# A perceiver block on one Trainium2 core: where the weights are quantised, two accumulator banks in the first unit, and the order of the drain

## The chip, the core and the metric

The kernel runs on one core of a Trainium2 chip. A core has a matrix engine (PE, with its weight loads shown apart as PEld), a vector engine (DVE), a scalar engine (ACT), a general engine (POOL) and a queue engine that mainly starts DMAs (SP). Each works through its own instructions in order and waits on semaphores for the others. Matrix products go to PSUM, which has eight banks of 128 x 512 floats; everything else lives in SBUF or in DRAM.

The metric is the time of one execution on the device, in microseconds (us). Three runs of the kernel before took 1754.26, 1755.36 and 1758.02 us; their median is 1755.36.

## The reference

The input is x (8 sequences of 64 rows, 512 wide) and a context (8 x 1601 rows, 256 wide). Three blocks follow each other, each with a residual sum:

```python
x = x + cross_attention(layernorm(x), ctx)       # 16 heads of 128; q and k normalised by RMS; softmax over 1601 keys
x = x + causal_self_attention(layernorm(x))      # 16 heads of 32
x = x + feed_forward(layernorm(x))               # 2048 wide, SiLU gate, RMS norm
```

The two weights of the feed-forward block are quantised inside the kernel, in groups of 64 along a row:

```python
w = w_fp32.astype(bfloat16); w_g = w.reshape(-1, 64)
scale = clip(mean(abs(w_g), axis=-1), 1e-08)
q = clip(round(w_g / scale), -1, 1)              # -1, 0 or 1
w_hat = q * scale;  w + (w_hat - w)              # the sum in bfloat16
```

## The kernel before

**Quantisation.** The two feed-forward weights are cut into 48 pieces of 128 x 512. For each piece `load_weights` (L332) loads it as floats into tile `wf` by SP; `magnitudes` (L343) makes |w| (`aw`) and sign(w) (`sg`) on ACT, in bfloat16; `quantise` (L350) makes the scales, the threshold mask `m`, mask times sign, and |w| - scale on DVE (tot, scl, thr, m, m, sg); `signed` (L369) finishes on DVE with two operations; `put_by` (L374) transposes the piece on DVE in blocks of 32 and sends it with four DMAs of SP to the DRAM tile `fw`. The feed-forward block reads `fw` back much later. The pieces are spread over the kernel wherever there is room: eight in the prologue, one for each pair of heads; in the main part one in the steps `q` = 0 and 4 of every unit, and in units 0 and 1 also in step 2; what is left, six, in the drain. The pool that holds `wf`, `aw`, `sg` and `m` has one buffer for each. It is `early` in the prologue and `fq` after it; `wpool[0]` names the one in use. The transposed piece is written over `aw`.

**Prologue.** Context tails and their key lengths first, then layer norm of x, then `two_heads(n)` (L505) for n = 0 to 8. It makes the queries of two heads with Strassen-Winograd products (q_u, q_2, q_5 in three banks), the copies p1, p5, u2 of partial sums on ACT, sums on DVE into `qraw` (L525, L533, L539), the lengths of the queries of the pair before (`query_roots`) and their products with the key weights (`score_weights`, tile `aps`, multiplied on DVE at L581). L539, the sum after the product of s3 and t3, must read q_u before the last product of the pair can use that bank. One piece is quantised within each call with n < 8; the load for the next call is issued after the call.

**Main part.** The cross attention runs in 16 units (8 sequences, 2 groups of 8 heads), each in six steps of 256 keys: 96 calls of `step(u, q)` (L1085). In a step PE forms the keys (seven products of 512 columns into banks p_u, p_5, p_2) to get their lengths, and the scores (seven of 256 columns, bank s_a); ACT squares the keys and sums them up (L741), DVE adds partial products (c12 L1158, c22 L1170, the quarters of the scores L1212 and L1222, c11 L1216). Scaling of the scores and the running maximum (`scale_pair`, L711, L727) are put off to the next step by the list `later`. Softmax and the weighted context of unit u - 1 run in the steps of unit u; its sums are gathered, inverted and divided in unit u + 1 (`find_sum`, `spread_sum`, `invert_sums`, `gather_first`, `gather`, `divide`). In unit 0 the steps 0 to 3 also hold the key lengths of the context tails for the second group (`tail_roots`, bank y0 or y1). PSUM has two banks m, and one each of k, s, y0, y1, y2 and y3. p_u takes bank k in every step; y0 to y3 hold the accumulators of the weighted context from unit 1 on.

**Drain.** After the last step: what is left of unit 14 (weighted context, gathering, division), the values of the first head group (`values`, tile `vp`), the softmax of unit 15 and its weighted context (L828), the rest of the pieces, and the loads of the weights that the later blocks need. Then the output projection (L1044), self attention and feed-forward.

**What sets the order.** In the prologue the instructions of PE, DVE and ACT run in the order in which the code writes them; in the main part POOL's too; from the drain on PE's alone. The other queues are ordered by the scheduler of the framework, with the semaphores for every dependency, a tile whose buffer is used again among them.

Of the kernel before, what the change touches and what calls it, by code (L numbers as in the profile page):

```python
# [19 lines left out]
P = 128  # L20
# [8 lines left out]
def perceiver_kernel(  # L29
# [313 lines left out]
    def magnitudes(wf):  # L343
        aw = wpool[0].tile([P, 8, 64], BF, tag="aw", name="aw")
        nc.scalar.activation(aw.rearrange("p g k -> p (g k)"), wf, AF.Abs)
        sg = wpool[0].tile([P, 8, 64], BF, tag="sg", name="sg")
        nc.scalar.activation(sg.rearrange("p g k -> p (g k)"), wf, AF.Sign)
        return aw, sg

    def quantise(u, aw, sg):  # L350
# [16 lines left out]
        return u, m, aw, sg  # L367

    def signed(u, m, aw, nd):  # L369
        nc.vector.tensor_tensor(nd, aw, nd, ALU.subtract)  # L370
        nc.vector.tensor_tensor(m, nd, m, ALU.mult)
        quantised[u] = m, aw

    def put_by(u):  # L374

        m, aw = quantised.pop(u)
        wT = aw.rearrange("p g k -> p (g k)")
        nc.vector.transpose(wT, m.rearrange("p g k -> p (g k)"))
# [10 lines left out]
    with tc.tile_pool(name="qphase", bufs=1) as qp, tc.tile_pool(  # L389
# [115 lines left out]
        def two_heads(n):  # L505
# [3 lines left out]
            if go:  # L509
# [14 lines left out]
                grow(q_2, a12, b21, True)  # L524
                nc.vector.tensor_tensor(qa[:, :NH], q_2, p1, ALU.add)  # L525
                grow(q_5, s1, t1, True)
                p5 = kept_q("qp5")
# [8 lines left out]
            if go:  # L536
                tern = quantise(n, *magnitudes(early.pop()))
                grow(q_u, s3, t3, False)
# [46 lines left out]
        with tc.manual_schedule(  # L585
# [72 lines left out]
            head_sums(0)  # L658
            early = [load_weights(0)]
            for n in range(H // 2 + 1):  # L660
# [5 lines left out]
                if n + 1 < H // 2:  # L666
                    early.append(load_weights(n + 1))
                if n == HG // 2:
# [7 lines left out]
    fq = xs.enter_context(tc.tile_pool(name="fq", bufs=1, side="right"))  # L676
    wpool[0] = fq

# [244 lines left out]

    def gather_first(u):

# [6 lines left out]
        nc.vector.tensor_tensor(p1, p6, p1, ALU.add)  # L932
        nc.gpsimd.tensor_tensor(cw[:, : W // 2], p1, p5, ALU.add)
        yG[u] = c15, cw

    def gather(u):

# [4 lines left out]
        (_, y12), (y21, y22) = outputs_of(u)  # L942
        add = nc.vector.tensor_tensor
        add(u3, p7, u2, ALU.add)
        add(y12, by_head(p4), by_head(u3), ALU.add)
        add(y21, by_head(p3), by_head(u4), ALU.add)
        add(u3, t22, u3, ALU.add)
        nc.gpsimd.tensor_tensor(y22, by_head(u3), by_head(p5), ALU.add)

    def divide(u):  # L950
        b, g = divmod(u, G)
        eng = nc.gpsimd if u < last - 1 else nc.vector
        for c in range(NC):
            y = a_sb[g][c][:, :, ts(b, S)]
            eng.tensor_tensor(y, y, rB[u], ALU.mult)

# [128 lines left out]
    def step(u, q):  # L1085
# [11 lines left out]
        fw_tile = None  # L1097
        tern = (q in TERN or u < 2 and q == 2) and n_q < NQ
        if tern:
            wf = load_weights(n_q)  # L1100


        p_u = bank("p_u", "k")
        product(p_u, a11, b11, True)
# [40 lines left out]
        if u > 1 and q == 2:  # L1145
            spread_sum(u - 2)
        if u == last and q == NQU - 1:
            spread_sum(last - 1)
        product(p_u, s2, t2_, False)
# [25 lines left out]
        if q == 1 and u > 1:  # L1175
            gather(u - 2)
        if u == last:
# [14 lines left out]
        if u > 1 and q in (2, 3):  # L1192
            for i in range(2):
                invert_sums(u - 2, 2 * (q - 2) + i)
        if u == last and q == NQU - 1:
            for i in range(4):
                invert_sums(last - 1, i)
        if n_tp < len(pairs) and turn_at[n_tp] == u * NQU + q:
# [27 lines left out]
        nc.scalar.copy(quarters[:, 2], s_a[:, 1])  # L1226
        squares(ssq[:, 0], 0, c11)
        if new:
            under_way = pair_products(*new)
            weigh(3)  # L1230
# [38 lines left out]
    with tc.manual_schedule(engines={mybir.EngineType.PE}):  # L1269
# [8 lines left out]
        prob_sums(last - 1, NQU - 1)  # L1278
        find_max(last)
        tail_products(last - 1)  # L1280
        mB[last] = spread_diag(mB[last])
        s_sb.pop((last - 1, NJF))
        under_way = pair_products(last - 1, NQU - 1)
        weigh(5)
        gather_first(last - 1)
        weigh(9)
        load_contexts(NU * NY)
        gather(last - 1)
        divide(last - 1)
        for h in range(HG // 2):  # L1290
# [533 lines left out]
```

## Time and profile before

| what | value |
|---|---|
| median of three runs | 1755.36 us |
| the profiled execution | 1753.64 us |
| its span, first to last instruction | 1751.8 us |
| mean granted clock of PE | 0.983 |
| PE, DVE, ACT, POOL busy | 95%, 74%, 66%, 59% |
| chain that ended last | PE 75%, DVE 9%, POOL 8%, ACT 4% |
| prologue's eight steps with a piece | 27.6 to 167.6 us |
| unit 0 | 178.0 to 254.9 us |
| last step, then drain | from 1418 us |

The span is cut into stages by the first products of each. A row of the timeline gives start, duration, engine, line, operation, the tile written and the tiles read, and in brackets how long the engine stood idle before and what released it. The busy share of PE is an average over stages with different limits. A granted clock under 1 means that PE ran at a lower rate for part of that stage.

### The profile page before, as it was taken

To read this page: it belongs to the slowest core of one execution; us is meant where nothing else is said; L and a number is where in the kernel's file an instruction comes from. 1 tells how busy PE (TensorE), PEld (TensorE's weight loads), DVE (VectorE), ACT (ScalarE), POOL (GpSimd) and SP (SyncE) were. 2 spreads that over 40 slices of the span, in tenths; PEclk is the share of its full clock that TensorE was granted. 3 is DMA by queue.
4 is the path that set the end of the run, shared out by engine and by line. 5 is a ranking of instruction groups with operands and counts; after the bars stand their busy time and mean duration, and the time that the engine had idled before them with its cause. 6 is when DMAs were issued, how large, how long until landed. Compare 5 with 4: busy or idle time off the path is not lost.

```text
span 1751.8 us, 22186 instructions
## 1 busy us (share of the span) xinstructions
PE 1671.6 (95%) x6068; PEld 1070.0 (61%) x6068; DVE 1293.2 (74%) x1937; ACT 1161.7 (66%) x4511; POOL 1027.8 (59%) x1240
## 2 busy tenths in 40 slices
PE   7768999999999999999999999999999988999999
PEld 4544446666666666666666666666666554466787
DVE  5555678888887878888888878888888878435641
ACT  4544778787777778787777878787777763113451
POOL 3120225687878697787878787787878771100031
PEclk9888999999999999999999999999999998999999
DMA  6111212121121121212121211121111116700340
GB/s 205 22 25 15 58 25 48 44 49 36 34 49 35 46 47 34 48 40 44 38 43 35 50 43 35 47 45 38 38 43 49 33 53 189 214 1 1 85 108 24
DMA packets 254243, 92.73 MB, mean 53 GB/s; under 512 B 208400, under 2 KB 234792, under 8 KB 254120
## 3 DMA queue, kind: packets, MB, share of 16 engines
q1 hardware_dynamic: 244762, 68.78, 17.7%
q0 software_dynamic: 8928, 22.02, 4.3%
q8 instruction: 48, 0.79, 0.2%
q14 instruction: 75, 0.61, 0.1%
q10 hardware_dynamic: 430, 0.53, 0.1%
HBM read 77.62 MB, written 7.34 MB: 49 GB/s over the span
## 4 chain that ended last, share of the span: by engine, by line
PE 75%; DVE 9%; POOL 8%; ACT 4%; issue 2%; DMA 1%; SPq 0%; DVEq 0%; ACTq 0%; POOLq 0%
PE p_u L737 15%; PE y L737 13%; PE p L737 11%; PE s_a L737 10%; PE gu L1635 3%; PE op L1044 3%; PE aps L580 2%; PE kp L302 2%; PE fop L1753 2%; PE s L737 2%; PE mm_qk L1430 2%; PE q_u L481 2%; PE q L481 1%; PE vp L1029 1%; POOL den L870 1%
## 5 line engine op out<-in xcount | busy, mean ns | idle before, releaser
L741 ACT ACTIVATE c<-c 128x128 f32<-128x128 f32 x1152 | 341.7, 302 | 94.3 <-DVE c L1170 70.5
L741 ACT ACTIVATION_READ_ACCUMULATOR c<-c 128x1 f32 x1152 | 220.9, 192 | 0.0
L737 PE MATMUL p_u<-wk,cxT 128*128 128x512 f32 x384 | 197.0, 594 | 6.5 <-ACT p_u L741 6.5
L711 DVE TENSOR_TENSOR s<-s,ssq 128x1024 f32<-128x1024 f32 x96 | 130.6, 1360 | 54.9 <-ACT ssq L105 54.9
L737 PE MATMUL y<-s,cxn 128*128 128x256 f32 x540 | 146.8, 381 | 0.0
L727 DVE TENSOR_TENSOR mx<-mx,s 128x512 f32<-128x512 f32 x160 | 137.3, 858 | 5.5
L737 PEld LDWEIGHTS s_a<-aT,cxS 128*128 128x128 f32 x384 | 73.5, 192 | 92.8 <-issue 81.7
L800 DVE TENSOR_TENSOR s<-s,mB 128x1024 f32<-128x1024 f32 (+1 forms) x102 | 125.4, 1241 | 1.6 <-ACT mB L778 1.6
L865 POOL TENSOR_TENSOR yT<-s 128x256 f32<-128x256 f32 x76 | 82.9, 1091 | 69.2 <-PE y L737 67.3
L741 ACT ACTIVATE p_u<-p_u 128x128 f32<-128x128 f32 x384 | 100.4, 262 | 27.2 <-PE p_u L737 18.1
L737 PE MATMUL s_a<-aT,cxS 128*128 128x256 f32 x384 | 115.1, 382 | 0.0
L804 ACT ACTIVATE s<-s,zero_t 128x1024 f32<-128x1024 f32 (+1 forms) x102 | 112.0, 1099 | 4.3 <-DVE s L800 4.3
L737 PE MATMUL s_a<-aT,cxT 128*128 128x256 f32 x384 | 114.3, 379 | 0.0
L737 PEld LDWEIGHTS y<-s,cxn 128*128 128x128 f32 x540 | 103.4, 191 | 14.6
L737 PE MATMUL p_u<-wkS,cxT 128*128 128x512 f32 x192 | 101.1, 608 | 5.9 <-DVE c L1170 5.9
L737 PEld LDWEIGHTS s_a<-aT,cxT 128*128 128x128 f32 x384 | 72.8, 190 | 51.2 <-issue 40.9
L1137 ACT COPY p<-p 128x512 f32<-128x512 f32 x96 | 56.2, 585 | 69.9 <-PE p L737 68.2
L737 PE MATMUL p_u<-wkS,cxS 128*128 128x512 f32 x192 | 99.7, 601 | 1.4 <-POOL cxS L230 1.4
L737 PE MATMUL p<-wkS,cxS 128*128 128x512 f32 x192 | 99.3, 599 | 1.4 <-POOL cxS L228 1.4
L737 PE MATMUL p<-wk,cxS 128*128 128x512 f32 x192 | 99.1, 598 | 0.0
L737 PE MATMUL p<-wk,cxT 128*128 128x512 f32 x192 | 98.0, 592 | 0.0
L1170 DVE TENSOR_TENSOR c<-p_u,p 128x512 f32<-128x512 f32 x96 | 63.7, 664 | 41.1 <-PE p_u L737 41.0
(272 smaller groups left out, 4338.7 us busy)
## 6 DMA issues: line engine op xcount, KB each, us to landing
cxn<-in_ctx_dram SPq DMA_DIRECT2D x96, 256.0 KB
cxB<-in_ctx_dram SPq DMA_DIRECT2D x192, 64.0 KB
wf<-in_L_ffn_w_gate_up_dram SPq DMA_DIRECT2D x32, 256.0 KB
fgu<-fw POOLq DMA_DIRECT2D x4, 2048.0 KB, 8.4
fw<-aw SPq DMA_DIRECT2D x192, 32.0 KB
wq<-in_L_xattn_Wq_dram SPq DMA_DIRECT2D x4, 1024.0 KB
wf<-in_L_ffn_w_proj_dram SPq DMA_DIRECT2D x16, 256.0 KB
wo<-in_L_xattn_Wo_dram POOLq DMA_DIRECT2D x16, 256.0 KB, 5.6
```

The lines of the kernel that those rows point to most:

```text
L481: nc.tensor.matmul(out_, a[:, c], b[:, c], start=first, stop=True, skip_group_check=not first)
L711: nc.vector.tensor_tensor(flat, flat, kr.unsqueeze(2).to_broadcast([P, 2 * HG, S]), ALU.mult)
L727: nc.vector.tensor_tensor(mx[u][:r], mx[u][:r], s[:r], ALU.max)
L737: nc.tensor.matmul(out_, a, w, start=start, stop=True, skip_group_check=not start)
L741: nc.scalar.activation(k[:, ts(h, HD)], k[:, ts(h, HD)], AF.Square, accum_out=ssq[:, 4 * half + h : 4 * half + h + 1],)
L800: nc.vector.tensor_tensor(t, t, m.to_broadcast([r, len(js), W]), ALU.subtract)
L804: nc.scalar.activation(t, t, AF.Exp, bias=zero_t[: t.shape[0]], scale=1.0)
L865: eng.tensor_tensor(s1, a21, a22, ALU.add)
L1044: nc.tensor.matmul(op, o_sb[h][:, ts(t, P)], wo_sb[h], start=(h == 0), stop=(h == H - 1),)
L1137: nc.scalar.copy(p5, p_5)
L1170: nc.vector.tensor_tensor(c22, p_u, p5, ALU.add)
L1635: nc.tensor.matmul(gu[:, cols], fgu_sb[rr // 8][:, rr % 8, c, :], xs_[n_][c][:, cols], start=(c == 0 and n_ == 0), stop=(c == ND - 1 and n ...
```

## The change

1. *Prologue.* `magnitudes` moves out of `two_heads`: it is called with the load, after the call before. `quantise` moves forward, to just after the first sum on DVE (L525). The transposed piece no longer goes over `aw`, but over `wf`, seen as bfloat16 (`wT`), as long as `wpool` has one entry.
2. *After the prologue.* `wpool` has two entries, so `aw` and `sg` get two buffers; the transposed piece goes over `aw` as before.
3. *Unit 0.* Every step takes a piece, six in place of three, so three are left for the drain. p_u takes bank y2 in odd steps of unit 0.
4. *Gathering.* `gather` adds y21 first and is a generator; in the steps it is run through at once. `gather_first` and `gather` take the engine for their one addition on POOL as an argument.
5. *Last step.* `spread_sum` and `invert_sums` of unit 14 move to the end of step (15, 5).
6. *Drain.* `find_max` and `spread_diag` of unit 15 move behind the products with the tails and three of the last seven products of unit 14. Gathering runs wholly on DVE and in two halves, each divided by itself (`divide_half`), the first ahead of the last product.

```diff
     def magnitudes(wf):
-        aw = wpool[0].tile([P, 8, 64], BF, tag="aw", name="aw")
+        n = len(wpool)
+        aw = wpool[0].tile([P, 8, 64], BF, tag="aw", name="aw", bufs=n)
         nc.scalar.activation(aw.rearrange("p g k -> p (g k)"), wf, AF.Abs)
-        sg = wpool[0].tile([P, 8, 64], BF, tag="sg", name="sg")
+        sg = wpool[0].tile([P, 8, 64], BF, tag="sg", name="sg", bufs=n)
         nc.scalar.activation(sg.rearrange("p g k -> p (g k)"), wf, AF.Sign)
-        return aw, sg
+        return aw, sg, wf.bitcast(BF)[:, :512] if n == 1 else aw.rearrange("p g k -> p (g k)")
...
     def put_by(u):
-        m, aw = quantised.pop(u)
-        wT = aw.rearrange("p g k -> p (g k)")
+        m, wT = quantised.pop(u)
         nc.vector.transpose(wT, m.rearrange("p g k -> p (g k)"))
...
                 nc.vector.tensor_tensor(qa[:, :NH], q_2, p1, ALU.add)
+                tern = quantise(n, *early.pop())
                 grow(q_5, s1, t1, True)
...
             if go:
-                tern = quantise(n, *magnitudes(early.pop()))
                 grow(q_u, s3, t3, False)
...
-            early = [load_weights(0)]
+            early = [magnitudes(load_weights(0))]
...
-                    early.append(load_weights(n + 1))
+                    early.append(magnitudes(load_weights(n + 1)))
...
-    wpool[0] = fq
+    wpool = [fq, fq]
...
+        add(y21, by_head(p3), by_head(u4), ALU.add)
+        yield
         add(u3, p7, u2, ALU.add)
         add(y12, by_head(p4), by_head(u3), ALU.add)
-        add(y21, by_head(p3), by_head(u4), ALU.add)
         add(u3, t22, u3, ALU.add)
-        nc.gpsimd.tensor_tensor(y22, by_head(u3), by_head(p5), ALU.add)
+        eng.tensor_tensor(y22, by_head(u3), by_head(p5), ALU.add)
...
+    def divide_half(u, j):
+        for y in [o[j] for o in outputs_of(u)]:
+            nc.vector.tensor_tensor(y, y, rB[u][:, 4 * j : 4 * j + 4], ALU.mult)
...
-        tern = (q in TERN or u < 2 and q == 2) and n_q < NQ
+        tern = (q in TERN or u == 1 and q == 2 or u == 0) and n_q < NQ
...
-        p_u = bank("p_u", "k")
+        p_u = bank("p_u", "y2" if u == 0 and q % 2 else "k")
...
-        if u == last and q == NQU - 1:
-            spread_sum(last - 1)
         product(p_u, s2, t2_, False)
...
-        if u == last and q == NQU - 1:
-            for i in range(4):
-                invert_sums(last - 1, i)
...
         squares(ssq[:, 0], 0, c11)
+        if u == last and q == NQU - 1:
+            spread_sum(last - 1)
+            for i in range(4):
+                invert_sums(last - 1, i)
...
-        find_max(last)
         tail_products(last - 1)
-        mB[last] = spread_diag(mB[last])
         s_sb.pop((last - 1, NJF))
         under_way = pair_products(last - 1, NQU - 1)
-        weigh(5)
-        gather_first(last - 1)
+        weigh(3)
+        find_max(last)
+        mB[last] = spread_diag(mB[last])
+        weigh(2)
+        gather_first(last - 1, nc.vector)
+        weigh(1)
+        g_last = gather(last - 1, nc.vector)
+        next(g_last)
+        divide_half(last - 1, 0)
         weigh(9)
         load_contexts(NU * NY)
-        gather(last - 1)
-        divide(last - 1)
+        for _ in g_last:
+            pass
+        divide_half(last - 1, 1)
```

More of the change, by code (lines that the diff above doesn't have):

```diff
@@ L343, in magnitudes, with quantise @@
     def magnitudes(wf):
-        aw = wpool[0].tile([P, 8, 64], BF, tag="aw", name="aw")
+        n = len(wpool)
+        aw = wpool[0].tile([P, 8, 64], BF, tag="aw", name="aw", bufs=n)
         nc.scalar.activation(aw.rearrange("p g k -> p (g k)"), wf, AF.Abs)
-        sg = wpool[0].tile([P, 8, 64], BF, tag="sg", name="sg")
+        sg = wpool[0].tile([P, 8, 64], BF, tag="sg", name="sg", bufs=n)
         nc.scalar.activation(sg.rearrange("p g k -> p (g k)"), wf, AF.Sign)
-        return aw, sg
-    def quantise(u, aw, sg):
+        return aw, sg, wf.bitcast(BF)[:, :512] if n == 1 else aw.rearrange("p g k -> p (g k)")
+    def quantise(u, aw, sg, wT):
         tot = small.tile([P, 8], F32, tag="tot", name="tot")
@@ L366, in quantise, with signed @@
         )
-        return u, m, aw, sg
-    def signed(u, m, aw, nd):
+        return u, m, aw, sg, wT
+    def signed(u, m, aw, nd, wT):
         nc.vector.tensor_tensor(nd, aw, nd, ALU.subtract)
         nc.vector.tensor_tensor(m, nd, m, ALU.mult)
-        quantised[u] = m, aw
+        quantised[u] = m, wT
     def put_by(u):
-        m, aw = quantised.pop(u)
-        wT = aw.rearrange("p g k -> p (g k)")
+        m, wT = quantised.pop(u)
         nc.vector.transpose(wT, m.rearrange("p g k -> p (g k)"))
@@ L922, in by_head, with gather_first @@
         return t.rearrange("p (h s) -> p h s", s=S)
-    def gather_first(u):
+    def gather_first(u, eng=nc.gpsimd):
         y0, y1 = yps[u][:2]
@@ L932, in gather_first, with gather @@
         nc.vector.tensor_tensor(p1, p6, p1, ALU.add)
-        nc.gpsimd.tensor_tensor(cw[:, : W // 2], p1, p5, ALU.add)
+        eng.tensor_tensor(cw[:, : W // 2], p1, p5, ALU.add)
         yG[u] = c15, cw
-    def gather(u):
+    def gather(u, eng=nc.gpsimd):
         c15, cw = yG.pop(u)
@@ L943, in gather @@
         add = nc.vector.tensor_tensor
+        add(y21, by_head(p3), by_head(u4), ALU.add)
+        yield
         add(u3, p7, u2, ALU.add)
         add(y12, by_head(p4), by_head(u3), ALU.add)
-        add(y21, by_head(p3), by_head(u4), ALU.add)
         add(u3, t22, u3, ALU.add)
-        nc.gpsimd.tensor_tensor(y22, by_head(u3), by_head(p5), ALU.add)
+        eng.tensor_tensor(y22, by_head(u3), by_head(p5), ALU.add)
     def divide(u):
         b, g = divmod(u, G)
-        eng = nc.gpsimd if u < last - 1 else nc.vector
         for c in range(NC):
             y = a_sb[g][c][:, :, ts(b, S)]
-            eng.tensor_tensor(y, y, rB[u], ALU.mult)
+            nc.gpsimd.tensor_tensor(y, y, rB[u], ALU.mult)
+    def divide_half(u, j):
+        for y in [o[j] for o in outputs_of(u)]:
+            nc.vector.tensor_tensor(y, y, rB[u][:, 4 * j : 4 * j + 4], ALU.mult)
     def find_sum(u):
@@ L1175, in step @@
         if q == 1 and u > 1:
-            gather(u - 2)
+            list(gather(u - 2))
         if u == last:
```

## The prediction

> **What bounds the kernel now.** I read the page first: the span and the busy shares.
>
> ```profile
> span 1751.8 us, 22186 instructions
> ...
> PE 1671.6 (95%) x6068; PEld 1070.0 (61%) x6068; DVE 1293.2 (74%) x1937; ACT 1161.7 (66%) x4511; POOL 1027.8 (59%) x1240
> ```
>
> TensorE is the bound of the main part, where the change does little. Its places have less PE: the prologue (27 to 178 us), unit 0 (178 to 254) and the drain (from 1418). Next, busy time by stage, a prologue step and two of unit 0 (length, then PE, PEld, DVE, ACT, POOL, clock, DMA):
>
> ```profile
> 99.40:116.60 17.20, 12.91 (x45) 8.34 (x44) 9.70 (x19) 8.36 (x16) 2.84 (x4) 0.90 0.14 23
> 191.40:204.90 13.50, 12.73 (x36) 6.70 (x36) 9.61 (x17) 9.91 (x46) 1.79 (x4) 1.00 0.13 20
> 204.90:218.40 13.50, 12.73 (x36) 6.70 (x36) 8.88 (x15) 10.91 (x48) 1.79 (x4) 1.00 0.29 50
> ```
>
> A prologue step leaves PE idle for 4 us, a step of unit 0 for 0.8. The table of waits names both:
>
> ```profile
> PE q_u L481 <- DVE qraw L539: 30.0, 7, 5.4
> ...
> PE p_u L737 <- ACT p_u L741: 4.7, 5, 1.5
> ```
>
> The timeline shows the prologue's order: the first load, issued at 35.53, releases ACT 2.87 us later; PE waits for L539, which stands on DVE behind the quantisation; the transpose (L378) and then its four stores come at the step's end, and the next step's first copy (L523) starts 0.55 us after the transpose has ended.
>
> ```profile
> 38.40 0.63 ACT L345 ACTIVATE aw<-wf 128x512 bf16<-128x512 f32 x1 [6.59 <-DMA wf<-in_L_ffn_w_gate_up_dram]
> ...
> 110.47 1.13 PE L481 MATMUL q_u<-xS,wq 128*128 128x256 f32 x4 [4.29 <-DVE qraw L539]
> ...
> 116.48 0.71 DVE L378 STREAM_TRANSPOSE aw<-m 128x512 bf16<-128x512 bf16 x1
> ...
> 117.74 0.37 ACT L523 COPY qp<-q_u 128x256 f32<-128x256 f32 x1 [4.42 <-PE q_u L481]
> ```
>
> In the drain, PE's three long waits, and what a store takes: transpose ends at 1506.09, ACT is released at 1510.35.
>
> ```profile
> 1427.86 0.47 PE L110 MATMUL bp<-denh,ones_r 128*128 128x512 f32 x1 [4.14 <-DVE st L699]
> ...
> 1444.83 0.66 PE L784 MATMUL tp_mx<-ident,mx 128*128 128x128 f32 x4 [3.79 <-DVE mx L727]
> ...
> 1456.99 5.08 PE L1029 MATMUL vp<-a,wv 128*128 128x512 f32 x8 [3.38 <-DVE a L955]
> ...
> 1510.35 0.63 ACT L345 ACTIVATE aw<-wf 128x512 bf16<-128x512 f32 x1 [1.00 <-DMA fw<-aw]
> ```
>
> The sum is made against the profiled run: 1753.64 us, of which 1751.8 are span; it is 1.7 below the median, 1755.36.
>
> **Prologue.** Two edits pull against each other. The DVE part of a quantisation goes ahead of two adds, so L539 no longer holds up PE: that frees the 4.29 us wait. But Abs and Sign become the last ACT instructions before the next step's first copy, and the transposed result now goes into wf, which has one buffer. So load n+1 must wait for the stores of piece n, Abs for the load, and behind Abs on ACT stand all three copies that PE and DVE need. What covered load and stores before was most of a step; now nothing covers them.
>
> Call T the end of the transpose and p the start of the step's first copy. T to p now: stores 4.26 (1506.09 to 1510.35; 4.42 after 1516.62), load 2.75 (2.87 in the row; packets of later loads end about 2.3 after issue, plus the 0.4 seen at 38.40), Abs and Sign 1.06 (38.40 to 39.46), 0.05 for the semaphore: 8.1 against 0.55.
>
> p to T, at full clock: copy 0.45; DVE: add 0.42, quantisation 3.0 (39.06 to 42.06), two adds 0.95, so the last group of q_u starts at 4.85 (PE's own groups take 4.1 from copy, 65.43 to 69.56, and are ready at 4.6). From there: group 0.86, two aps 1.9, second multiply 0.65, two sign operations 0.92, transpose 0.71: 5.05. Sum 9.9. But PE has then stood idle for some 6 us (its three early groups end 2.2 after T; the copy lands at 8.5), and its groups come back slow: after 8.97 us idle at 42.53 three groups took 1.45, 1.71 and 1.37 instead of 0.86, 1.95 lost; at 92.22 (5.37 idle) the way from group to T took 7.76 instead of 5.05, 2.7 lost. I take 2.3, of which 2.0 reach the path: p to T is 11.9. The Trainium skill's page "TensorE: Matmul & The Clock Gate", section "Part 1: The HAM clock gate", says that an idle window of about 3.4 us halves the clock until some 3.4 us of work have passed, and so speaks against an edit that opens such a gap; by its figure the loss would be an estimated 1.7 a step and the prologue some 4 us shorter than my sum.
>
> So a period is 8.1 + 11.9 = 20.0; before it was (151.56 - 46.35)/6 = 17.5. Step 0: its load still lands at 38.40, so its first copy moves from 28.85 to 39.46, and the second step's p from 46.35 to about 55.2: +8.85. Six periods: +15.0. The last step has no load behind it and gains 17.1 - 11.9 = 5.2. Prologue: **+18.7**. Bounds: +3.3 if the clock never drops (period 18.0), +26 with stores and load at 9 and p to T at 12.2.
>
> **Unit 0.** A second bank frees PE from waiting for the squares of p_u: 0.79, 0.80, 0.80, 0.79, 1.47 and 0.80 us at the six step ends, 5.45 in all. The three extra pieces cost ACT 1.06 each, which fits into waits of 1.44 before L310, and DVE 4.5 each (signs and transpose 1.55, quantisation 2.95). From the quarter add (L1222) to the c12 add (L1158) DVE now has 4.85 + ssq 0.6 + scale 1.25 + two maxima 1.4 = 8.1; before 7.9 in steps 1 to 3. There PE still gains about 0.9 a step. In steps 4 and 5 there is no key work: L1158 came 6.3 after the quarter add and now comes 7.5 after it; the piece at the end of step 5 puts 2.9 of DVE ahead of the scores that find_max waits for. These two give back some 2.5. I take **-1**; bounds -5.45 and +3 (one quantisation that nothing hides). The three stores more per unit (2.6 us of SP each) lie in steps where SP is idle half of the time.
>
> **Main part.** The order in gather is new in 14 units: y21 first needs POOL's add, 0.73 to 1.57 long from 346.1, and the gather starts at 348.8: hidden. Should it not be, 14 x 0.5.
>
> **Last step and drain.** spread_sum moves to the end of step (15, 5): PE goes on at 1423.6 instead of waiting for denl. DVE still has scale, maxima and tail until 1428.4, so L1158 comes at 1428.4 instead of 1431.45, and without the reciprocals (3.38) ahead of it L1170 at 1429.1 instead of 1435.35: the step's PE work ends some 6 us earlier. The reciprocals now stand after the squares of c11, wait for the copy of rB (about 1435.2), end at 1438.6, and behind them on DVE stand the signs, transpose (1.5), scale (1.25) and maxima (1.5): tp_mx at about 1442.9, only 1.9 earlier. That is the new wait, some 4.7 us, behind which now stand only four products and not tail plus seven. Then gather_first on DVE (copy 0.6, three adds 1.2), y21 0.4, two half divisions 0.85: values start at about 1448.7 instead of 1456.99, -8.3, if the first four heads need only their half; if they wait for both halves, 2.5 later. Of the slow and broken first heads (5.08 instead of 3.44, 0.58, 0.74) I count 1.7 as gone, since three pieces fewer stand among DVE's copies. Together **-10**; bounds -6 and -14. Later the loads of context (PE waits 1.89 at 1485.64) follow the buffers and shift with them.
>
> Sum: 1753.64 + 18.7 - 1 - 10 = 1761.3.
>
> **Rivals.**
> A. The clock holds through the new wait, so p to T is 9.9: prologue +3.3, sum 1746. For it: the groups at 110.47 and 127.66 took 1.13 and 1.17 after 4.29 idle. Against: both steps still show 0.90, and 42.53 shows half rate. It turns to faster where the prologue costs under 7.5, a period under about 18.4.
> B. The drain gives nothing: tp_mx waits as long as before behind the reciprocals and both halves are waited for. Then -1 to -3 there: 1769 to 1771. For it: the chain on DVE is only 1.9 shorter.
> C. Unit 0 gives its full 5.4 and the drain 14, at +18: 1753, no change. Against: DVE's 8.1.
> D. The load does not wait for the stores, so the edit does more than I read: seven waits of 4.29 go, -30 there before step 0's +7: about 1720. Against: one buffer.
>
> **How the numbers follow.** Forecast 0.42 (own range 1757 to 1766), A 0.17, B 0.20, C 0.16, D 0.05. The band of 0.2% is about 3.5 us, the spread of the three runs and about what a measurement of this kernel can tell. Slower: 0.40 of the forecast and B, 0.60. Same: 0.02 and 0.14 of C, 0.16. Faster: A, D and 0.02 of C, 0.24. The range 1747 to 1772 leaves out D, most of A and the top of B.
>
> **What would show it.** Prologue: ACT idle 7 to 8 us before L345, released by the load; no PE wait for L539; periods near 20; PEclk lower. Unit 0: no PE wait for p_u; L1158 later after the quarter add. Drain: no wait before bp; tp_mx waiting over 3 us; vp near 1449 plus the earlier shift. The forecast falls if prologue periods are under 18.4 or the drain's waits stay.

## The result and the profile after

The changed kernel takes 1767.52 us (median of three runs, 1765.85 to 1769.82) against 1755.36 us before; the ratio is 1.0067, with a 95% interval of 1.0042 to 1.0093. It is slower by 0.7%. (One execution of the first run with whole divisions, below, took 4452 us and is left out of its times.) The profiled execution is the longest of the three, 1769.82 us, 16.2 us above the profiled one of before, and all stage times below are from that pair. The page of the kernel after: its span, busy time by engine, and the granted clock in 40 slices, in tenths (slice 2 stands at 7 where it was 8; slices 3 and 4 stand at 8 as before; the 8 that stood in the drain, in slice 34, is gone).

```profile
span 1768.0 us, 22174 instructions
...
PE 1673.8 (95%) x6068; PEld 1075.4 (61%) x6068; DVE 1291.5 (73%) x1941; ACT 1158.3 (66%) x4511; POOL 1022.7 (58%) x1238
...
PEclk9788999999999999999999999999999999999999
```

TensorE's busy time as a whole has hardly changed (1671.6 before), but that is a sum of two opposites: from 27.6 us to the start of unit 0 it is 118.3 instead of 110.5, with a granted clock of 0.82 instead of 0.86, and in the drain it is less. The rest of the loss is in waits. Setting each step of the two traces beside its counterpart shows where the 16.2 us arise; the shift is how much later the same instruction starts.

| place | shift there | what the stage added | forecast |
|---|---|---|---|
| unit 0 begins (178.0 before, 202.3 after) | +24.2 | prologue +24.2 | +18.7 |
| step (1,3), after the last extra piece's work | +26.6 | units 0 and 1 +2.4 | -1 |
| tail product of the last step (L690) | +26.1 | 13 units between: -0.4 | 0 |
| second group of the out-projection (L1048) | +15.8 | last step and drain -10.3 | -10 |
| end of the execution | +16.2 | +0.4 | 0 |

In the prologue the timeline shows the order that was forecast: the transpose into wf, its four stores, the load that waits for them, Abs, and only then the step's first copy, for which TensorE has been waiting.

```profile
110.31 0.71 DVE L378 STREAM_TRANSPOSE wf<-m 128x512 bf16<-128x512 bf16 x1
...
111.05 2.59 SPq L381 DMA_DIRECT2D fw<-wf  x4
...
115.31 0.33 SPq L340 DMA_DIRECT2D wf<-in_L_ffn_w_gate_up_dram  x1
118.02 0.63 ACT L346 ACTIVATE aw<-wf 128x512 bf16<-128x512 f32 x1 [7.56 <-DMA wf<-in_L_ffn_w_gate_up_dram]
...
119.07 0.35 ACT L523 COPY qp<-q_u 128x256 f32<-128x256 f32 x1
...
119.57 2.04 PE L481 MATMUL q_u<-xS,wqS 128*128 128x256 f32 x4 [6.24 <-ACT qp L523]
```

The transpose ends at 111.02 and the first copy starts at 119.07: 8.05 us. The load is issued at 115.31, 4.3 after the transpose. The group at 119.57 takes 2.04 us where one at full clock takes 1.03; the granted clock is 0.50 from 118.5 to 125.3. Two lines of the table of waits (sum, times, longest) and two steps by stage (length; PE, PEld, DVE, ACT, POOL; clock) give the size over the prologue:

```profile
ACT aw L346 <- DMA wf<-in_L_ffn_w_gate_up_dram: 61.9, 8, 10.3
...
PE q_u L481 <- ACT qp L523: 45.4, 7, 7.2
```

```profile
99.00:118.90 19.90, 14.08 (x44) 9.77 (x44) 9.24 (x18) 7.83 (x16) 4.03 (x5) 0.84 0.10 21
119.30:139.20 19.90, 14.17 (x44) 9.81 (x44) 9.86 (x19) 7.76 (x16) 4.59 (x8) 0.84 0.12 20
```

The old wait for L539 is gone, a longer one stands in its place, the clock of a step fell from 0.90 to 0.84, and TensorE is busy for 14.1 us of a step instead of 12.9. Step (1,0) is where the units lose most. Before, and then after: the step's first product, the root that ends the key norms, the scaling, and the transposed maxima.

```profile
254.68 1.13 PE L737 MATMUL p_u<-wk,cxT 128*128 128x512 f32 x2 [0.80 <-ACT p_u L741]
...
256.77 0.31 ACT L105 ACTIVATE ssq<-ssq,zero_t 128x16 f32<-128x16 f32 x1
...
257.12 1.23 DVE L711 TENSOR_TENSOR s<-s,ssq 128x1024 f32<-128x1024 f32 x1 [1.26 <-ACT ssq L105]
...
259.85 0.66 PE L784 MATMUL tp_mx<-ident,mx 128*128 128x128 f32 x4 [0.17 <-DVE mx L727]
```

```profile
277.21 1.02 PE L737 MATMUL p_u<-wk,cxT 128*128 128x512 f32 x2
...
280.14 0.67 PE L737 MATMUL s_a<-aT,cxS 128*128 128x256 f32 x2 [1.05 <-ACT s L1225]
...
281.87 0.31 ACT L105 ACTIVATE ssq<-ssq,zero_t 128x16 f32<-128x16 f32 x1
...
282.52 1.22 DVE L711 TENSOR_TENSOR s<-s,ssq 128x1024 f32<-128x1024 f32 x1
...
285.25 0.66 PE L784 MATMUL tp_mx<-ident,mx 128*128 128x128 f32 x4 [0.98 <-DVE mx L727]
```

From the step's start to the maxima it is 8.0 instead of 5.2 us: ACT's roots end 2.6 later, and on DVE a quantisation (from 279.27) ends just as the scaling could start, so both engines are late together. TensorE pays for it in three waits: 1.05 for ACT's copy of the scores, which stands behind the squares, 0.45 for its copy at L1116 (neither stood there before), and 0.98 for the maxima (0.17 before). Last, the drain after. No wait stands before the sums' bank; the maxima still wait, and the values start at 1475.08, which is 18.1 later than before where the step began 26.1 later.

```profile
1470.13 1.08 PE L784 MATMUL tp_mx<-ident,mx 128*128 128x128 f32 x4 [3.73 <-DVE mx L727]
...
1475.08 1.10 PE L1033 MATMUL vp<-a,wv 128*128 128x512 f32 x2 [0.89 <-DVE a L959]
1476.65 6.28 PE L1033 MATMUL vp<-a,wv 128*128 128x512 f32 x14 [0.48 <-DVE a L959]
```

### The profile page after: what moved, and what is told of

Same layout as the page of the kernel before. It is cut to its first block, busy times and chain, and to the rows that moved or that the text cites. A ratio compares the mean times of both kernels' runs of the same rounds, so it can differ in the third digit from the quotient of the medians.

```text
span 1768.0 us, 22174 instructions
## 1 busy us (share of the span) xinstructions
PE 1673.8 (95%) x6068; PEld 1075.4 (61%) x6068; DVE 1291.5 (73%) x1941; ACT 1158.3 (66%) x4511; POOL 1022.7 (58%) x1238
## 4 chain that ended last, share of the span: by engine, by line
PE 66%; DVE 12%; POOL 9%; ACT 6%; issue 4%; DMA 3%; SPq 1%; DVEq 0%; POOLq 0%; ACTq 0%
PE p_u L737 13%; PE y L737 11%; PE p L737 9%; PE s_a L737 9%; PE gu L1644 3%; PE op L1048 3%; PE q_u L481 2%; PE fop L1762 2%; PE mm_qk L1439 2%; PE s L737 2%; ACT c L741 2%; DVE s L711 2%; PE vp L1033 2%; DMA wf<-in_L_ffn_w_gate_up_dram 1%; ACT p_u L741 1%
## 5 line engine op out<-in xcount | busy, mean ns | idle before, releaser
L865 POOL TENSOR_TENSOR yT<-s 128x256 f32<-128x256 f32 x76 | 77.1, 1014 | 69.5 <-PE y L737 68.2
```

The costliest lines, as they stand in the source:

```text
L865: eng.tensor_tensor(s1, a21, a22, ALU.add)
```

## The experiments

My theory: most of the loss is the prologue's, because the load waits for the stores and TensorE's clock falls in the wait; units 0 and 1 lose because of the extra pieces, not the second bank; the drain gives 10. The rivals stand in each expectation. Ratios are to the kernel before, on the same chip. In the later tables "drain" is the time from the tail product of the last step to the second group of the out-projection; it is 99.21 before and 88.86 after. About half of that difference is the clock: in these stretches TensorE's busy time falls from 84.99 to 79.96 for the same work, and its granted clock rises from 0.93 to 0.98.

**The prologue's old order.**

```diff
-        return aw, sg, wf.bitcast(BF)[:, :512] if n == 1 else aw.rearrange("p g k -> p (g k)")
+        return aw, sg, aw.rearrange("p g k -> p (g k)")
...
-                tern = quantise(n, *early.pop())
...
+                tern = quantise(n, *magnitudes(early.pop()))
                 grow(q_u, s3, t3, False)
...
-            early = [magnitudes(load_weights(0))]
+            early = [load_weights(0)]
...
-                    early.append(magnitudes(load_weights(n + 1)))
+                    early.append(load_weights(n + 1))
```

> The changed kernel with the prologue's order of before: the load is taken up in the middle of the step, the transposed piece lies in aw. My theory (the prologue costs 24.2 us in the two traces, unit 0 and 1 together 2.4, and the drain gives 10): unit 0 begins within 1 us of 178.0, its first step of unit 2 comes 2 to 3 us later than before, the whole is 1753.6 + 2.4 - 10 = 1746, a ratio of 0.995 to the kernel before. Rival: the slower part lies behind the prologue (the drain gives nothing by itself and the profiled 10 us are a shift that the late start made possible): 1756, ratio 1.001.

Measured: 1744.9 us, ratio 0.9947 (0.9930 to 0.9964); expected 1746. Unit 0 begins at 176.7, 1.3 before the 178.0 of the kernel before where within 1 was expected, and the drain takes 88.63, as in the changed kernel. The rest of the change is thus a gain of some 0.5% by itself, and the prologue is what turns it into a loss; the rival falls.

**The load freed of the stores.** The signed piece goes into aw and is transposed into m; nothing is larger, and wf is free as soon as Sign has read it.

```diff
-        return aw, sg, wf.bitcast(BF)[:, :512] if n == 1 else aw.rearrange("p g k -> p (g k)")
+        return aw, sg, None if n == 1 else aw.rearrange("p g k -> p (g k)")
...
+        if wT is None:
+            nc.vector.tensor_tensor(aw, nd, m, ALU.mult)
+            quantised[u] = aw, m.rearrange("p g k -> p (g k)")
+            return
```

> The changed kernel, but in the prologue the signed piece goes into aw and is transposed into m, so that the next load needs no store to have ended; it still stands behind the issue of four stores on SP's queue. My theory (load waits for the stores of the piece): from the end of the transpose to the first copy 2.6 for the four issues, 2.75 for the load and 1.06 for Abs and Sign = 6.4 instead of 8.05, period some 18.4 instead of 20.3, the whole 1767.5 - 13 = 1754. Rival (the load starts when it does for another reason, the queue or the order on ACT): the period stays at 20.3, 1767.

Measured: 1712.3 us, ratio 0.9760 (0.9745 to 0.9774): some 54 us under the changed kernel, where I expected 13. The timeline of this version:

```profile
85.10 0.71 DVE L382 STREAM_TRANSPOSE m<-aw 128x512 bf16<-128x512 bf16 x1
...
85.84 2.59 SPq L385 DMA_DIRECT2D fw<-m  x4
85.85 0.63 ACT L346 ACTIVATE aw<-wf 128x512 bf16<-128x512 f32 x1 [1.30 <-DVE m L382]
...
86.91 0.35 ACT L527 COPY qp<-q_u 128x256 f32<-128x256 f32 x1
...
88.54 0.55 SPq L340 DMA_DIRECT2D wf<-in_L_ffn_w_gate_up_dram  x1
```

Abs waits for DVE's transpose alone; the load that it reads was there long before. I had left the load behind the issue of the four stores. But SP's order is not written by hand in this kernel. Once the load needed no store, the planner (the framework's scheduler) put the second load ahead of the first stores on SP, and every later load comes a step early. The period is 12.6 us (74.36, 86.91, 99.47), the clock of a step 1.00, and unit 0 begins near 145 instead of 202. So the theory's cause held (with the wait for the stores all of the loss goes, and more), and its size failed: it took SP's order as fixed.

**The load issued a step ahead by hand**, on the version with the freed load.

```diff
             early = [magnitudes(load_weights(0))]
+            ahead = [load_weights(1)]
...
-                    early.append(magnitudes(load_weights(n + 1)))
+                    early.append(magnitudes(ahead.pop()))
+                if n + 2 < H // 2:
+                    ahead.append(load_weights(n + 2))
```

> As the one before, and the load of piece n+1 is issued at the beginning of step n, when Sign of piece n has read wf, so that neither stores nor load stand between the transpose and the first copy; Abs and Sign keep their place ahead of the first copy. My theory: transpose to first copy about 1.2, TensorE is then the bound of a step (12.9 us busy), period 13.2 to 14.0, first copy still near 40, unit 0 begins near 155, the whole 1767.5 - 47 = 1720. Rival (the two places on ACT are the cost, or the stores now hold up the comparison that writes m): period 16 or more, the whole above 1740.

Measured: 1713.0 us, ratio 0.9762 (0.9747 to 0.9778), period 12.6 (86.0, 98.5, 111.3 at Abs); expected 1720 and 13.2 to 14.0. The same SP order as in the run before, and the same time: this says again that the first copy needs only the transposed piece out of the way. The rival (1740 or more) falls. Abs and Sign ahead of the copies cost nothing measurable here: TensorE's waits behind the first step are 8.9 us for L543 (7 waits) and 1.1 for the first copy.

**TensorE kept busy in the wait, too long**, by products whose result nothing reads, in the changed kernel.

```diff
+                if n > 0:
+                    idle_products(13, [P, 4, P])
```

> The changed kernel with 13 products of 128x512 whose result nothing reads, about 5.6 us of TensorE work, laid into TensorE's wait for the first copy in the seven later steps. My theory (of the 12.3 us from first copy to transpose some 2.4 are TensorE's lowered clock after 6.2 us idle): they become 9.9 to 10.2, the clock of the prologue's slices rises to 0.95 or more, the period is 18.0, the whole 1767.5 - 16 = 1751. Rival (the 12.3 come from the order on DVE, the quantisation ahead of two additions, or from the copies): they stay at 12, the whole 1767 or more.

Measured: 1780.8 us, ratio 1.0148 (1.0133 to 1.0163), slower than the changed kernel. The expectation is wrong by my sizing: a 128x512 product of this type is two passes of 0.43 us, so 13 took 11.2 us (the trace shows 26 passes) and outlasted the wait of 6.2. The trace is still of use: from the first group after them to the end of the transpose it was 8.98 us (105.46 to 114.44), against 11.77 in the changed kernel (99.25 to 111.02).

**TensorE kept busy for 5.2 us.** The same edit with 6.

> The changed kernel with 6 unread products of 128x512 in TensorE's wait, instead of the 13 that turned out to be two passes each, 0.86 us a product, and to outlast the wait: 5.2 us of work in a wait of 6.2. In the run with 13 the way from TensorE's first group after the wait to the end of the transpose was 8.98 us at full clock, against 11.77 in the changed kernel. My theory (the clock costs 2.8 us in each of seven steps): first copy to transpose 9.5, period 17.6, the whole 1767.5 - 19.5 = 1748. By the page's half rate over 3.4 us the loss would be 1.7 a step and the whole 1755.5. Rival (the unread products only shift the work behind them): 1765 or more.

Measured: 1750.1 us, ratio 0.9978 (0.9968 to 0.9989), against 1767.5 without the unread products. The first group after the wait, and two steps by stage (columns as above):

```profile
94.06 1.10 PE L481 MATMUL q_u<-xS,wqS 128*128 128x256 f32 x4 [0.97 <-ACT qp L523]
```

```profile
93.80:111.40 17.60, 16.52 (x56) 10.01 (x56) 9.06 (x18) 8.08 (x17) 4.03 (x5) 1.00 0.13 23
111.50:128.90 17.40, 16.51 (x56) 10.01 (x56) 9.68 (x19) 8.08 (x17) 4.62 (x8) 1.00 0.13 24
```

The clock is 1.00 in both, the period 17.5 to 17.9 from here on, first copy to transpose 9.56 instead of 12.27: the clock cost 2.7 us a step. Nothing else was changed, load and stores least of all (transpose to first copy is 7.9 to 9.0, and 8.0 to 8.6 in the changed kernel). One of the seven steps is an exception: before the group at 74.89 a wait of 2.03 us was left, the clock fell to 0.5 for 3.4 us, and that step took 19.2. The Trainium skill's page "TensorE: Matmul & The Clock Gate", section "Part 1: The HAM clock gate", has half rate for some 3.4 us, by which I estimated 1.7; the trace shows a longer stretch, 5.7 us from the first group on: in the changed kernel the groups at 119.57, 121.41 and 123.97 took 2.04, 1.91 and 1.71, and 1.02 only at 126.42. It also shows rival A of the prediction carried out: with the clock held the change is a small gain.

**The second bank without the extra pieces**, on the version with the freed load.

```diff
-        tern = (q in TERN or u == 1 and q == 2 or u == 0) and n_q < NQ
+        tern = (q in TERN or u < 2 and q == 2) and n_q < NQ
```

> On the kernel with the piece transposed into m (1712.3): the two banks in turn stay, but unit 0 takes the three pieces of before, in steps 0, 2 and 4, and six are left to the drain. My theory (TensorE's wait for the squares is worth 0.8 to 1.5 a step, and the pieces in consecutive steps cost 2.9 us in the first step of unit 1 and about 1 in each of steps 4 and 5): the steps of unit 0 take 12.5, 12.5, 12.5, 12.5, 11 and 11, the first two of unit 1 11 and 10.7, so that unit 2 begins 5 us or more earlier in relation to unit 0 than with six pieces; the drain with three pieces more gives back 0 to 2; the whole 1707 to 1710. Rival (the loss in unit 1 comes from the second bank, which lets TensorE run ahead of ACT): the first step of unit 1 keeps its 13.2 and the whole stays at 1712.

**The extra pieces without the second bank**, on the same version.

```diff
-        p_u = bank("p_u", "y2" if u == 0 and q % 2 else "k")
+        p_u = bank("p_u", "k")
```

> On the same kernel: six pieces in unit 0, but p_u always in the one bank of before. My theory: TensorE waits for the squares of p_u again, 0.8 or more in each step, the steps 0 to 3 take 13.5, and the loss of 2.9 in the first step of unit 1 stays, since it is on DVE and ACT: the whole 1712.3 + 4 to 6 = 1717. Rival (the second bank causes the loss in unit 1): the steps of unit 1 are those of before and the whole is 1715 or less.

The lengths of the steps, from TensorE's first product of one to that of the next, tell the two edits apart ("both" is the changed kernel; the version with the freed load has the same to 0.05):

| step | 0,0 | 0,1 | 0,2 | 0,3 | 0,4 | 0,5 | 1,0 | 1,1 | sum |
|---|---|---|---|---|---|---|---|---|---|
| before | 13.42 | 13.53 | 13.53 | 13.52 | 10.85 | 11.80 | 10.93 | 10.54 | 98.1 |
| bank alone | 12.46 | 12.46 | 12.47 | 12.46 | 10.17 | 11.47 | 12.47 | 10.54 | 94.5 |
| pieces alone | 13.43 | 13.52 | 13.53 | 13.52 | 11.91 | 12.68 | 11.99 | 11.68 | 102.3 |
| both | 12.46 | 12.47 | 12.46 | 12.89 | 12.05 | 12.62 | 13.80 | 11.70 | 100.5 |

and the drain takes 94.98 with the bank alone (six pieces left to it), 88.82 with the pieces alone and 88.96 with both (three left).

Over the eight steps the bank gives 3.6 and the three pieces cost 6.0 beside it; counted the other way round, the pieces cost 4.1 by themselves and the bank gives 1.8 beside them. The loss of 2.9 in step (1,0) is split: 1.5 of it come with the bank alone, 1.1 with the pieces alone, and the 1.2 of step (1,1) with the pieces alone. So neither expectation was right about that step, and the rival, by which the loss in unit 1 is the bank's, holds for 1.5 of its 4.0 us; over the eight steps the pieces are the loss. But "bank alone" is no faster as a whole (1714.5 us, 0.9770, 0.9755 to 0.9786), against my 1707 to 1710: the three pieces, left to the drain, cost 6.0 there, not 0 to 2. The values begin as early as with three (28.86 us after the tail product, and 28.85), and then TensorE waits longer for a load of context and twice for DVE. About half of the 6.0 is again the clock, which is 0.95 in this drain and 0.98 with three pieces (TensorE busy 82.81 and 79.90). TensorE in the drain with six pieces, and with three:

```profile
1439.97 12.14 PE L832 MATMUL y<-s,cxn 128*128 128x512 f32 x24 [2.77 <-DMA cxn<-in_ctx_dram]
...
1463.09 2.84 PE L1037 MATMUL vp<-a,wv 128*128 128x512 f32 x6 [1.06 <-DVE a L984]
1467.66 10.57 PE L1037 MATMUL vp<-a,wv 128*128 128x512 f32 x24 [1.74 <-DVE o_h L1048]
```

```profile
1444.28 10.54 PE L832 MATMUL y<-s,cxn 128*128 128x512 f32 x24 [1.71 <-DMA cxn<-in_ctx_dram]
...
1463.71 13.90 PE L1037 MATMUL vp<-a,wv 128*128 128x512 f32 x32
```

So moving three pieces from the drain to unit 0 moves 6 us from one place to the other. "Pieces alone" (1715.7 us, 0.9774, 0.9757 to 0.9791; expected 1717, the rival 1715 or less) can't be told from 1712.3 by its whole time within a few us; its eight steps are 1.8 us longer.

**The sums' spreading and reciprocals at their old places**, on the same version.

```diff
             spread_sum(u - 2)
+        if u == last and q == NQU - 1:
+            spread_sum(last - 1)
         product(p_u, s2, t2_, False)
...
+        if u == last and q == NQU - 1:
+            for i in range(4):
+                invert_sums(last - 1, i)
...
-        if u == last and q == NQU - 1:
-            spread_sum(last - 1)
-            for i in range(4):
-                invert_sums(last - 1, i)
```

> On the same kernel: the spreading of the last-but-one unit's sums and their reciprocals at their places of before, the rest of the drain as changed. My forecast made the maxima 1.9 us earlier through this edit and put the larger part of the 8.3 us at the values on the fewer products and half divisions: the wait for the bank comes back (some 4 us), the wait for the maxima shrinks, the values begin 2 us later, the whole 1714. Rival (the wait taken from the middle of the step is worth itself): values 4 to 6 us later, the whole 1717.

Measured: 1721.1 us, ratio 0.9811 (0.9788 to 0.9834). TensorE in the last step and drain:

```profile
1400.10 0.77 PE L110 MATMUL bp<-denh,ones_r 128*128 128x512 f32 x1 [5.72 <-DVE st L703]
...
1419.83 0.66 PE L788 MATMUL tp_mx<-ident,mx 128*128 128x128 f32 x4 [2.37 <-DVE mx L731]
...
1423.88 1.10 PE L1037 MATMUL vp<-a,wv 128*128 128x512 f32 x2 [1.67 <-DVE a L963]
```

The wait for the bank is back, 5.72. The tail product is at 1390.78 here and at 1388.48 with the edit, the values at 1423.88 and 1417.33: 4.25 later by the edit, and the drain takes 93.10 instead of 88.96. The rival's 4 to 6 holds, my 2 does not. The whole shows more than the edit: of the 6.1 us between the profiled executions 2.4 lie in the prologue, where nothing was changed.

**Whole divisions before the values**, on the same version, run twice.

```diff
-        next(g_last)
-        divide_half(last - 1, 0)
         weigh(9)
...
+        divide_half(last - 1, 0)
         divide_half(last - 1, 1)
```

> On the kernel with the piece transposed into m (1712.3): both halves are gathered and divided before the first values, the rest of the drain as changed. My forecast put 2.5 us on it (values of the first four heads need only their half): values begin 2.5 to 3 us later, the whole 1715. Rival (TensorE has the last products to do until then, or what the values gain is lost at the loads of context): less than 1 us at the context's products, the whole 1712.

> The same kernel as in the run with whole divisions, whose profiled execution was disturbed throughout and whose times (0.9774 of before, interval 0.975 to 0.980) can't tell 2.5 us. From the trace: with the products of the last-but-one unit ended at the same place, the values begin 2.5 to 3 us later than with half divisions (my forecast's 2.5), and the products with the context as much later. Rival: less than 1 us is left at the products with the context.

Measured: 1715.9 us, ratio 0.9774 (0.9750 to 0.9797), and 1715.4 us, ratio 0.9762 (0.9745 to 0.9778). From tail product to values it is 28.83 in the second run, and 28.85 without the edit: no difference. It doesn't test the claim, though. In the drain only TensorE's order is by hand; DVE's is the planner's, which put the divisions (L963) between the sums of the gathering, in the same order as without the edit:

```profile
1419.78 0.41 DVE L963 TENSOR_TENSOR a<-a,rB 128x256 f32<-128x256 f32 x1
1420.11 0.41 DVE L937 TENSOR_TENSOR cw<-c 128x256 f32<-128x256 f32 x1
1420.44 0.41 DVE L950 TENSOR_TENSOR cw<-y,c 128x256 f32<-128x256 f32 x1
1420.78 0.41 DVE L948 TENSOR_TENSOR a<-y,cw 128x256 f32<-128x256 f32 x1
1421.11 0.41 DVE L951 TENSOR_TENSOR a<-y,cw 128x256 f32<-128x256 f32 x1
1421.44 0.41 DVE L963 TENSOR_TENSOR a<-a,rB 128x256 f32<-128x256 f32 x1
```

What halves are worth as against one whole division per matrix (128x512) stays open.

**All six pieces into the main part**, on the version with the bank alone.

```diff
-        tern = (q in TERN or u < 2 and q == 2) and n_q < NQ
+        tern = (q in TERN or u < 8 and q == 2) and n_q < NQ
```

> On the kernel with the second bank and three pieces in unit 0 (1714.5): a third piece also in units 2 to 7, at step 2, so that none is left to the drain. My theory (three pieces cost 6.0 us in unit 0 and 6.2 in the drain by the two traces, because neither has DVE time to spare; a step of the later units has 2 us and the next 2.7): six pieces cost up to 0.3 each there, unit 0 keeps its gain of 6, and the drain is no later than with three pieces: the whole 1703 to 1708. Rival (4.5 us of DVE more in a step with 10.2 of 12.5 busy stall TensorE): 1 to 2 us a piece, the whole 1712 or more.

Measured: 1719.5 us, ratio 0.9790 (0.9766 to 0.9814); expected 1703 to 1708. The eight steps of units 0 and 1 keep their 6.0, the drain falls to 86.77 with no piece left to it, but units 2 to 7 take 18.2 us longer, 3.0 a piece. TensorE in step (3,2):

```profile
424.00 1.70 PE L741 MATMUL p_u<-wkS,cxT 128*128 128x512 f32 x2 [1.88 <-DVE c L1176]
```

The 2 us of DVE time that a step has over are not where the quantisation stands: behind its 2.9 us stand the additions that TensorE needs next. The rival holds. About half of the cost is the clock. Each of the six units has this wait of 1.88 us once. In units 3 to 7 the granted clock then stands at 0.5 for 3.4 us (424.4 to 427.8 behind the row above, whose group takes 1.70 us instead of 1.02), and these units take 3.2 to 3.5 longer; in unit 2 the clock stays at 1.00 behind the same wait, and the unit takes 1.4 longer. With the clock held, a piece would so cost an estimated 1.4, as the rival had it.

**The prologue's pieces in steps 1 to 7**, on the version with the freed load; one piece more is left to the drain.

```diff
-                tern = quantise(n, *early.pop())
+                tern = quantise(n - 1, *early.pop()) if n > 0 else None
...
-                signed(*tern)
-                put_by(n)
+                if n > 0:
+                    signed(*tern)
+                    put_by(n - 1)
...
-            early = [magnitudes(load_weights(0))]
+            early = []
...
-                    early.append(magnitudes(load_weights(n + 1)))
+                    early.append(magnitudes(load_weights(n)))
...
-    n_tp, n_q, n_cx = 1, H // 2, 0
+    n_tp, n_q, n_cx = 1, H // 2 - 1, 0
```

> On the kernel with the piece transposed into m (1712.3): the prologue takes its pieces in steps 1 to 7 instead of 0 to 7, so that the first copy of step 0 doesn't wait for the first load; one piece more is left to the drain. My theory (the first step's wait for the load costs 11 us at the first copy, of which 4 come back since TensorE has run ahead): first copy near 29, last first copy near 118 instead of 124.7, two of it lost to the fourth piece of the drain: the whole 1707. Rival (the step is bound by the loads of weights for the queries or by TensorE's groups): last first copy at 122 or later, 1712.

Measured: 1703.0 us, ratio 0.9702 (0.9682 to 0.9721), the fastest here: 3.0% under the kernel before. Expected 1707; the rival (1712) falls. The step's first copies at both ends of the prologue:

```profile
29.17 0.37 ACT L527 COPY qp<-q_u 128x256 f32<-128x256 f32 x1
41.42 0.35 ACT L527 COPY qp<-q_u 128x256 f32<-128x256 f32 x1
...
117.85 0.35 ACT L527 COPY qp<-q_u 128x256 f32<-128x256 f32 x1
```

The last first copy comes 6.8 earlier (124.65 before this edit), as forecast, and the drain takes 89.02 with four pieces against 88.96 with three: the fourth is free. With six it was 94.98, so the cost sets in with the fifth or sixth; the first three together cost 2.2 (86.77 with none).

## Why the prediction was right, and where it was not

The sign and the mechanism were right, and 1767.5 lies in the range and outside the forecast's own 1757 to 1766. The sum said 7.7 us more, and the pair of profiled executions shows 16.2 (the medians 12.2). Three terms follow, by its steps.

**Prologue, +18.7 forecast, +24.2 measured; mechanism shown.** Transpose to first copy was 8.05 (8.1 said). First copy to transpose was 12.27 instead of 11.9: the clock's share was sized at 2.0 and is 2.7 by the run with six unread products (which leaves 9.56 for the rest, 9.9 said), so the six periods were 20.5 instead of 20.0 and add 2.8, the last step 0.5. The first step added 1.1 more, and 1.35 are the first load's landing, 39.75 in this execution instead of 38.40; over the other runs of the study Abs of the first piece started between 38.1 and 39.2, so this term is mostly scatter of one execution. Of "what would show it", the wait of ACT for the load (7.6), the period and the lower clock came as written. One of its readings is off: at 42.53 the three groups follow each other after 1.87, 1.71 and 1.16 us, 2.1 lost, where it has 1.45, 1.71 and 1.37 and 1.95 lost; the 2.3 that it took is hardly touched by that. Its lower bound does not come out of its own terms: with a period of 18.0 they give +4.7 (8.85 + 3.0 - 7.2) and not +3.3, and the run with six unread products shows +4.9.

**Unit 0, -1 forecast, +2.4 measured; this step failed.** The gains of steps 0 to 3 were said to be 0.9 each and were 3.7 in sum; steps 4 and 5, together with the piece that is still open at the end of step 5, were to give back 2.5, and steps 4 and 5 gave back 2.0. What the step left out is unit 1: (1,0) lost 2.9 and (1,1) 1.2. I had counted the open piece as DVE time ahead of the scores and had not followed ACT, whose roots are 2.6 late there: TensorE, no longer held by the squares, starts (1,0) while ACT still has them to do, and the extra piece's Abs and Sign as well. By the runs: bank -3.6, and the pieces beside it +6.0.

**Last step and drain, -10 forecast, -10.3 measured; right in sum by luck, wrong in its parts.** The maxima were to come 1.9 earlier and came 0.8 earlier (23.9 instead of 24.7 after the tail product). The values came 8.05 earlier (8.3 said). But the sums' move is worth 4.2, where I gave it 2. And the three pieces that left the drain are worth 6.0 at the out-projection, where I gave them 1.7. What I had put down to DVE's copies there, the slow first heads, is in part the clock: it was at 0.93 in this stretch and is at 0.98, which TensorE's busy time shows as 5.0 of the 10.3, and no term of the sum was for it. The two make 10.2 of the 10.3, if they add; what is left for the maxima's place, the gathering and the halves is near nothing by the out-projection, though at the values they must have given the other 3.8, which six pieces would have eaten again. That is a difference and not a run of its own, so the parts behind the 3.8 stay open.

**Main part, 0 forecast**, -0.4 measured. The new order in gather is hidden.

**The rivals.** B (drain gives nothing) gave the time nearest to the measured one, and for a wrong reason: the drain gave all that was forecast. A is what happens when TensorE is kept awake. Summed anew from their own terms, B is 1768 to 1770 and C 1752, a us under what stands there. D was excluded by wf's one buffer, and the version that removes this reason shows that D's gain was there to be had: 1712.3 is below the 1720 that D was given.

The account of the 16.2 us is then: prologue +24.2, bank -3.6, three pieces +6.0 in units 0 and 1 and -6.0 in the drain, sums -4.2, all else -0.2. Bank and pieces are split in the order of the runs above, and the two parts of the drain are taken to add.

## What to carry to other kernels

A one-buffer tile that gets a second use couples what was apart: here a load, which nothing had needed in a hurry, came to stand behind four stores and ahead of every copy of the step. Ask of each reused tile who writes it next, and whether a tile that is dead by then could take the result; here one was, and it was worth some 54 us. And before work is moved from a crowded stage to another, price a piece in both: three pieces cost 6 us in either place, while a third in a later unit cost 3.0 each and a fourth in the drain none. Count a wait of TensorE twice, by its length and by what the clock loses behind it: in the prologue the second part was 2.7 us a step, and in the drain and the later units about half of what such waits cost.

## What the runs showed of the hardware

After 6.2 us without products TensorE ran at half rate (granted clock 0.50) for 5.7 us of nearly unbroken work (groups of 2.04, 1.91 and 1.71 us instead of 1.03, from 119.57 to 125.3), which cost 2.7 us a step; a gap of 0.97 us left the next group at 1.10. Much shorter waits can be enough: with all pieces in the main part a wait of 1.88 us was followed by 3.4 us at 0.5 in five units of six and by none in the sixth, and with six unread products a wait of 2.03 us was and one of 2.19 us was not. The stretches at 0.5 in these traces last 3.4, 6.8 or 10.2 us. Unread products in the wait, 5.2 us of them, brought the ratio from 1.0067 to 0.9978, some 16 us, without moving a load or a store. The loads stood ahead of stores on SP once no tile forbade it, which is the planner's doing and not the chip's; the run with the freed load was 42 us faster than its forecast, which had taken the old order.
